# Weights of edges read by VectorE straight from the PSUM bank of the turned logits, in a graph-attention layer on one core

## The chip, the core and the metric

The kernel runs on one core of one Trainium2 chip. The metric is the device time of one execution in microseconds (us); lower is better. A time is the median of several executions, and the profile shows one execution of its own.

The core's engines have their own instruction queues, each worked off in order: TensorE (PE; its weight loads are listed as PEld), VectorE (DVE), ScalarE (ACT), GpSimd (POOL) and SyncE (SP). They wait for each other by semaphores. Data lies in SBUF, with 128 partitions, or in PSUM, where TensorE writes its products; PSUM consists of banks, and one bank holds 512 float32 numbers per partition.

## The reference, cut to what matters

```python
h = relu(layernorm(x))                          # 12500 nodes x 256
q, k, v = h @ Wq + bq, h @ Wk + bk, h @ Wv + bv # 8 heads of 32
logits  = einsum('ehd,ehd->eh', q[dst], k[src]) / sqrt(32)
seg_max = segment_max(logits, dst)
expv    = exp(logits - seg_max[dst])
denom   = segment_sum(expv, dst)
attn    = expv / denom[dst]
agg     = segment_sum(attn[:, :, None] * v[src], dst)
out     = agg + (h @ Wskip + bskip)
y       = h + gelu(out)
return x + layernorm(y) * gamma + beta
```

There are 200,000 edges, sorted by `dst`; `src` is random. So each edge fetches a row of k and v from anywhere, and its sums go to one of a few neighbouring nodes.

## The kernel before, in words

A first stage computes h and the tables of k and v and of q in DRAM. The last stage finishes what is left. Between them lies the *walk* over the edges, most of the span, and the change is there.

**Tiling.** The sorted edges are cut into S = 8 streams of NST = 66 steps. One step takes from each stream K = 3 tiles of 128 edges (two in the last step). An edge is a partition: a tile `kv` of 128 x 8 streams x 512 numbers holds k (first 256) and v (last 256) of 128 edges of each stream.

**One step c**, for its tiles j = 0, 1, 2:

- `gather` (L1027): GpSimd issues eight indirect DMAs per tile, two steps ahead, into one of six `kv` buffers; `gather_next(c, j)` fetches tile j of step c+2 into the buffer that `weigh(c, j)` has done with.
- `hot_e`, `hot_n` (L1042 to L1055): TensorE and ScalarE make 0/1 matrices that say which node an edge belongs to, `to_e` (node to edge) and `to_n` (edge to node).
- `spread` (L1065): TensorE spreads q over the edges, into PSUM (`ps_qe`); `times` (L1074): VectorE multiplies it into k, in place; `total` (L1081): VectorE reduces to logits `L`, 64 per edge partition (8 streams x 8 heads).
- `turn` (L1091): TensorE transposes the logits of a tile into the PSUM tile `ps_x`, partitions 0 to 63, 128 columns per tile. For j = 0 ScalarE then puts the previous step's last maximum into column 0 (L1093).
- `maxima` (L1102 to L1105): VectorE scans along the edges forward and backward, with `pen` marking the borders of nodes (scratch in partitions 64 to 127 of `ps_x`), and subtracts the maxima: `W`. `exponent` (L1109): ScalarE.
- `turn_back` (L1117): TensorE transposes the weights back to edges as partitions, 64 columns per tile, into columns 0 to 191 of `ps_x`.
- `weights` (L1125): ScalarE copies these 128 x 192 numbers into the SBUF tile `w`.
- `carried` (L1131, L1133): ScalarE copies what the previous step carried over (`wden`), and the weights of tiles 1 and 2 into the head columns of the products `vw`, since they also sum up to the denominators.
- `weigh` (L1140): VectorE multiplies v by the weights, broadcast over the 32 numbers of a head, into `vw`; for tile 0 a small multiply by `wden` follows (L1145).
- `add_up` (L1164): TensorE sums the products by nodes into `ps_a` (streams in group i = 0 and 2) and `ps_hot` (i = 1); ScalarE copies the sums (L1176) and puts the unfinished last node of each stream into the first row of the next step's tile (L1182); SyncE stores the sums.

Beside this a *pair* of finished node blocks is completed in about every 39/32 steps: divide (L841 to L855), skip product (L849, L862, L866), add (L871), gelu (L875), statistics (L878 on), and in the following step normalisation and scaling (L898 to L914).

**What sets the order.** No scheduler: the helper `keep` chains every instruction to the one before on its engine, so each engine's order is the order of the program text. The loop over c interleaves three steps by hand. In short: `times`, `total`, `turn` of (c, 2); `weigh(c-1, 2)`; `maxima(c)`; sums of c-1; `exponent(c)`; `turn_back(c)`; `weights(c)`; `carried(c)`; `times`, `total` of (c+1, 0); `weigh(c, 0)`; `hot_n(c)`; `turn(c+1, 0)`; the pair's middle part and `hot_e(c+2)`; `times`, `total`, `turn` of (c+1, 1); `weigh(c, 1)`; the rest of `hot_e(c+2)`; sums of (c, 0 and 1). Waits between engines come from the tiles: whoever reads a tile waits for its last writer, and a writer for its last readers, tracked by tile.

The buffers that matter: `w` has one, `ps_x` comes from a pool with one buffer, a whole bank; `turn(c, 0)` takes it anew in each step.

Of the kernel before, what the change touches and what calls it, by code (L numbers as in the profile page):

```python
# [28 lines left out]
F32 = mybir.dt.float32  # L29
# [11 lines left out]
P = 128  # L41
HEADS = 8
# [4 lines left out]
S = 8  # L47
K = 3
CH = K * P
# [709 lines left out]
def walk_streams(tc, N, HID, NST, KL, many, ident, idx, d0_row, slot_row, near, near_n, e_tab, pen_tab, h_tab,  # L759
# [6 lines left out]
    nc = tc.nc  # L766
# [3 lines left out]
    SH = S * HEADS  # L770
# [6 lines left out]
    def keep(ins):  # L777

        before = latest.get(ins.ins.engine)
        if before is not None:  # L780
            tc.add_manual_dep(ins.ins, before, mybir.DependencyInfo(
                mybir.DependencyClass.NoSync, mybir.DependencyReason.DATA), reason="kept order")
        latest[ins.ins.engine] = ins.ins.name
        return ins
# [167 lines left out]
    with ExitStack() as es:  # L952
        def pool_of(name, bufs, **kw):
            return es.enter_context(tc.tile_pool(name=name, bufs=bufs, **kw))
# [6 lines left out]
        work = pool_of("work", 2)  # L961
# [3 lines left out]
        xt_ps = pool_of("xt_ps", 1, space=PSUM)  # L965
# [22 lines left out]
        def tiles_of(c):  # L988
            return KL if c == NST - 1 else K


        step = [dict() for _ in range(NST + 3)]

        def where(s):
# [91 lines left out]
        def turn(c, j):  # L1086

            g = step[c]
            if j == 0:
                g["xt"] = xt_ps.tile([P, 512], F32, name="ps_x")  # L1090
            keep(nc.tensor.transpose(g["xt"][:SH, j * P:(j + 1) * P], g["L"][:, j, :], ident))  # L1091
            if j == 0:
                keep(nc.scalar.copy(g["xt"][:SH, 0:1],  # L1093
                                    low0 if c == 0 else step[c - 1]["M"][:, CH - 1:]))

        def maxima(c):
            g = step[c]
            n = tiles_of(c) * P
            X, R, pen = g["xt"][:SH, :n], g["xt"][SH:, :n], g["pen"]
            M = g["M"] = work.tile([SH, CH], F32, name="M")[:, :n]  # L1100
            W = g["W"] = work.tile([SH, CH], F32, name="W", bufs=1)[:, :n]
            keep(nc.vector.tensor_tensor_scan(R, pen[:SH, :n], X, -BIG, op0=OP.add, op1=OP.max))  # L1102
            keep(nc.vector.tensor_tensor_scan(mirrored(M, 0, n), mirrored(pen[SH:, :], 1, n),
                                              mirrored(R, 0, n), -BIG, op0=OP.add, op1=OP.max))
            keep(nc.vector.tensor_tensor(W, X, M, op=OP.subtract))  # L1105

        def exponent(c):
            W = step[c]["W"]
            keep(nc.scalar.activation(W, W, AF.Exp))  # L1109

        def turn_back(c):
            g = step[c]

            n = tiles_of(c)
            ps = g["xt"][:, :K * SH].rearrange("p (k n) -> p k n", k=K)
            for j in range(n):
                keep(nc.tensor.transpose(ps[:, j, :], g["W"][:, j * P:(j + 1) * P],  # L1117
                                         ident[:SH, :SH]))

        def weights(c):  # L1120
            g = step[c]
            n = tiles_of(c)
            ps = g["xt"][:, :K * SH].rearrange("p (k n) -> p k n", k=K)
            g["w"] = work.tile([P, K, SH], F32, name="w", bufs=1)
            keep(nc.scalar.copy(g["w"][:, :n, :], ps[:, :n, :]))  # L1125

        def carried(c):

            g = step[c]
            g["vw"] = [work.tile([P, S, SUMS], F32, name="vw", bufs=K) for _ in range(K)]  # L1130
            keep(nc.scalar.copy(wden[c % 2][0:1], g["kv"][0][0:1, :, HID - HEADS:HID]))  # L1131
            for j in range(1, tiles_of(c)):
                keep(nc.scalar.copy(g["vw"][j][:, :, :HEADS],  # L1133
                                    g["w"][:, j, :].rearrange("p (s h) -> p s h", s=S)))

        def weigh(c, j):
            g = step[c]
            t = g["vw"][j]
            wj = g["w"][:, j, :].rearrange("p (s h) -> p s h", s=S)
            keep(nc.vector.tensor_tensor(  # L1140
                t[:, :, HEADS:].rearrange("p s (h d) -> p s h d", h=HEADS),
                wj[:, :, :, None].to_broadcast([P, S, HEADS, D]),
                g["kv"][j][:, :, HID:].rearrange("p s (h d) -> p s h d", h=HEADS), op=OP.mult))
            if j == 0:
                keep(nc.vector.tensor_tensor(t[:, :, :HEADS], wj, wden[c % 2], op=OP.mult))  # L1145
# [100 lines left out]
        for c in range(NST - 1):  # L1246

            pair_next = None
            if c in due:
                pair_next = Pair(fin, due[c][0],  # L1250
                                 lambda: hot_ps.tile([P, 2, KC, P], F32, name="ps_hot"),
                                 lambda: ag_ps.tile([P, 2 * HID], F32, name="ps_a").rearrange(
                                     "p (b d) -> p b d", b=2),
                                 keep)
            if c + 2 < NST:
                windows(c + 2)
            for half in range(2):
                times(c, K - 1, half)
                spread(c + 1, 0, half)
            total(c, K - 1)  # L1260
            turn(c, K - 1)
            if c:
                weigh(c - 1, K - 1)
                gather_next(c - 1, K - 1)
            maxima(c)
            if before:
                before.factors()
            if c:
                add_up(c - 1, 0, range(K - 1, K))
                add_up_products(c - 1, 1)  # L1270
            exponent(c)
            turn_back(c)
            if c:
                add_up_results(c - 1, 1)
            weights(c)
            if c:
                add_up(c - 1, 2)
            carried(c)
            for half in range(2):
                times(c + 1, 0, half)  # L1280
                spread(c + 1, 1, half)
            total(c + 1, 0)
            weigh(c, 0)
            gather_next(c, 0)
            for j in range(K):
                hot_n(c, j)
            turn(c + 1, 0)
            if before:
                before.normal()
                before.shifted()  # L1290
            if pair:
                pair.turn()
                pair.divisors()
                pair.divide()
                pair.skip()
            if before:
                before.scale()
                before.store(0)
                before.store(1)
            if pair_next:  # L1300
                pair_next.fetch()
            if c == NST - 2:
                for i in range(4):
                    last(i)
            if c + 2 < NST:
                for i in range(QT // 2):
                    hot_e(c + 2, i)
            if pair:
                pair.add()
                table_of(AF.Gelu)  # L1310
                pair.gelu()
            for half in range(2):
                times(c + 1, 1, half)
                if tiles_of(c + 1) == K:
                    spread(c + 1, K - 1, half)
            total(c + 1, 1)
            turn(c + 1, 1)
            weigh(c, 1)
            gather_next(c, 1)
            if c + 2 < NST:  # L1320
                for i in range(QT // 2, QT):
                    hot_e(c + 2, i)
            add_up(c, 0, range(K - 1))
            if c + 2 < NST:
                penalties(c + 2)
            if c + 3 < NST:
                prefetch(c + 3)
            if c == NST - 2:
                weigh(c, K - 1)
                add_up(c, 0, range(K - 1, K))  # L1330
                add_up(c, 1)
                if pair_next:
                    pair_next.turn()
                    pair_next.skip()
            if pair:
                table_of(AF.Sqrt)
                pair.stats()
                pair.root()
                table_of(AF.Exp)
            if c == NST - 2:  # L1340
                add_up(c, 2)
            before, pair = pair, pair_next
            if c > 1:
                step[c - 2] = None

        c = NST - 1
# [14 lines left out]
        if before:  # L1361
            before.factors()
        turn_back(c)
        weights(c)
        carried(c)
        weigh(c, 0)
        if pair:
# [53 lines left out]
        if extra:  # L1421
            with tc.If(many > 0):
                for m in extra:
                    p = Pair(fin, m, lambda: hot_ps.tile([P, 2, KC, P], F32, name="ps_hot"),
                             lambda: ag_ps.tile([P, 2 * HID], F32, name="ps_a").rearrange(
                                 "p (b d) -> p b d", b=2), lambda ins: ins)
# [349 lines left out]
```

## Time and profile before

| | |
|---|---|
| median of 6 runs | 2954.03 us (2933.71 to 2965.32) |
| the profiled execution | 2965.96 us, its span 2964.2 us |
| mean granted TensorE clock in it | 0.678 |
| instructions in it | 29239 |
| data from and to HBM | 538.91 MB read, 108.23 MB written, 218 GB/s |
| `times` L1074 on VectorE | 394 of 1218 ns, 465.2 us |
| `total` L1081 on VectorE | 197 of 2286 ns, 450.4 us |
| `weigh` L1140 on VectorE | 197 of 2285 ns, 450.1 us |
| gathers L1027 on GpSimd | 1576 of 1099 ns, 1731.3 us |

A group of the profile is written as line, engine, operation, output <- inputs, shapes, x count; then the busy time in us, the mean of one in ns, and after a second bar the time in which the engine stood idle just before such an instruction, with what ended it. "remote" is a releaser that the profile can't name, "issue" stands for no wait that the profile shows. A wait line gives total us, how often, and the longest. A timeline line gives start and duration in us, and in brackets the idle time before it. Matmul ends are modelled.

### The profile page before, as it was taken

What the parts mean: (1) busy time and instruction counts of PE and PEld (TensorE: products, weight loads), DVE (VectorE), ACT (ScalarE), POOL (GpSimd) and SP (SyncE); (2) the same over time, 40 slices, a digit from 0 to 9 for tenths busy, and PEclk for the clock granted to TensorE, in tenths of its full rate; (3) what the DMA queues carried; (4) which work ended last, traced back from release to release, by engine and by line L of the source; (5) the groups of instructions that cost most, each with busy time, mean ns of one, the idle gap of its engine ahead of it and who ended that gap; (6) DMA issues with size and microseconds to landing.
All of it is one profiled execution on the core that took longest, in us unless ns stands there. A gap on an engine that the chain in (4) does not pass through costs nothing.

```text
span 2964.2 us, 29239 instructions
## 1 busy us (share of the span) xinstructions
PE 1796.3 (61%) x7824; PEld 941.0 (32%) x7824; DVE 1989.8 (67%) x2330; ACT 1099.8 (37%) x2552; POOL 1868.7 (63%) x1745
## 2 busy tenths in 40 slices
PE   6899824445454756565565556667665666555556
PEld 3455412212232323233233323333332333223333
DVE  7777546666575767667666667767776766756774
ACT  3333212222243434434334434334344444334343
POOL 4423557776775766677576676676766776756750
PEclk9999856665576566656766666665666666666677
DMA  7766766676776777777677777787776776867762
GB/s 249 266 236 254 255 187 206 204 214 201 220 232 192 226 229 224 207 228 226 194 223 219 222 233 226 223 241 226 231 222 204 234 226 210 251 186 225 228 196 86
DMA packets 306127, 649.33 MB, mean 219 GB/s; under 512 B 52836, under 2 KB 192238, under 8 KB 300954
## 3 DMA queue, kind: packets, MB, share of 16 engines
q0 software_dynamic: 128768, 423.23, 48.5%
q1 hardware_dynamic: 176434, 223.46, 22.9%
q8 instruction: 65, 1.06, 0.1%
q14 instruction: 112, 0.92, 0.1%
q10 hardware_dynamic: 748, 0.66, 0.1%
HBM read 538.91 MB, written 108.23 MB: 218 GB/s over the span
## 4 chain that ended last, share of the span: by engine, by line
PE 26%; another core or an unknown queue 20%; issue 17%; ACT 12%; DVE 11%; POOL 8%; DMA 4%; SPq 1%; DVEq 0%; POOLq 0%; ACTq 0%
POOL kv L1027 7%; PE ps_kv L256 4%; PE ps_a L1164 4%; DVE vw L1140 3%; ACT kv L1182 3%; DVE kv L1074 3%; PE ps_qe L1065 3%; PE ps_a L866 3%; PE ps_hot L908 2%; PE ps_q L262 2%; DMA kv<-kv_tab,idx 2%; PE ps_hot L1164 2%; ACT to_e L1044 2%; PE ps_hot L1053 1%
## 5 line engine op out<-in xcount | busy, mean ns | idle before, releaser
L1027 POOL DMA_INDIRECT kv<-kv_tab,idx x1576 | 1731.3, 1099 | 794.7 <-issue 456.0
L1140 DVE TENSOR_TENSOR vw<-w,kv 128x2048 f32<-128x2048 f32 x197 | 450.1, 2285 | 414.1 <-ACT kv L1182 288.8
L1074 DVE TENSOR_TENSOR kv<-ps_qe,kv 128x1024 f32<-128x1024 f32 x394 | 465.2, 1218 | 97.6 <-remote 42.6
L1081 DVE TENSOR_REDUCE L<-kv 128x64 f32<-128x2048 f32 x197 | 450.4, 2286 | 6.9 <-issue 0.2
L1164 PE MATMUL ps_a<-vw,to_n 128*32 128x264 f32 (+1 forms) x2344 | 322.8, 556 | 103.0 <-DVE vw L1140 58.0
L1065 PE MATMUL ps_qe<-qw,to_e 64*128 64x256 f32 (+1 forms) x1576 | 319.8, 403 | 106.5 <-issue 83.5
L1053 PE MATMUL ps_hot<-near_n,et 48*128 48x384 bf16 x197 | 71.5, 400 | 455.5 <-issue 200.8
L1176 ACT COPY sums_w<-ps_a 128x264 f32<-128x264 f32 x130 | 49.4, 380 | 786.6 <-remote 441.9
L1044 ACT ACTIVATE to_e<-ps_hot,ones 128x384 fp32r<-128x384 f32 x396 | 213.2, 579 | 338.8 <-PE ps_hot L1042 147.8
L1065 PEld LDWEIGHTS ps_qe<-qw,to_e 64*128 64x128 f32 (+1 forms) x1576 | 230.1, 256 | 266.5 <-issue 203.5
L1042 PE MATMUL ps_hot<-et,near 48*128 48x384 bf16 x396 | 144.5, 417 | 119.8 <-issue 83.3
L1164 PEld LDWEIGHTS ps_a<-vw,to_n 128*32 128x32 f32 (+1 forms) x2344 | 113.4, 153 | 308.4 <-issue 169.8
L256 PE MATMUL ps_kv<-w_kv,hT 128*128 128x512 f32 x392 | 192.4, 612 | 17.2 <-ACT hT L141 15.5
L268 POOL TENSOR_TENSOR qp<-qp 128x256 fp32r<-128x256 f32 x98 | 88.5, 903 | 167.5 <-ACT qp L267 167.1
L1164 PE MATMUL ps_hot<-vw,to_n 128*64 128x264 f32 x808 | 188.5, 616 | 8.7 <-issue 8.2
L1091 PEld LDWEIGHTS ps_x<-ident,L 128*64 128x64 f32 x197 | 24.6, 125 | 511.5 <-issue 475.5
L1102 DVE TENSOR_TENSOR_SCAN ps_x<-pen,ps_x 64x384 f32<-64x384 f32 x66 | 63.0, 955 | 177.3 <-remote 123.0
L986 ACT ACT_TABLE_LOAD x138 | 177.1, 1283 | 2.4
L1117 PE MATMUL ps_x<-ident,W 64*128 64x64 f32 x197 | 35.4, 309 | 214.0 <-ACT W L1109 153.2
L866 PE MATMUL ps_a<-w_s,hT 128*128 128x256 f32 x368 | 144.9, 562 | 11.1 <-issue 3.3
L1055 ACT ACTIVATE to_n<-ps_hot,ones 128x384 f32<-128x384 f32 x197 | 107.0, 579 | 105.7 <-remote 91.2
L1182 ACT COPY kv<-ps_a 1x264 f32<-1x264 f32 x388 | 143.2, 369 | 6.3
(279 smaller groups left out, 2229.2 us busy)
## 6 DMA issues: line engine op xcount, KB each, us to landing
qw<-q_pc SPq DMA_DIRECT2D x264, 128.0 KB
kv<-kv_tab,idx POOLq DMA_INDIRECT x1576
kv_tab<-kvo SPq DMA_DIRECT2D x16, 1280.0 KB
q_pc<-qp SPq DMA_DIRECT2D x16, 1280.0 KB
qw<-q_pc SPq DMA_DIRECT2D x264, 64.0 KB
table<-sums_w SPq DMA_DIRECT2D x264, 61.9 KB
pen<-pen_tab SPq DMA_DIRECT2D x66, 192.5 KB
sums<-table SPq DMA_DIRECT2D x92, 132.0 KB
```

The lines of the kernel that those rows point to most:

```text
L256: ins = nc.tensor.matmul(ps_kv, hT[:, c, :], w_kv[:, c, :], start=c == 0, stop=c == KC - 1)
L866: self.keep(nc.tensor.matmul(self.ps[:, b, :], self.hT[:, b, c, :], w_s[:, c, :], start=False, stop=False, skip_group_check=True))
L986: keep(nc.scalar.activation(dummy[:, 1:2], dummy[:, 0:1], function))
L1027: nc.gpsimd.indirect_dma_start(out=t[:, s, :], out_offset=None, in_=kv_tab[:, :], in_offset=bass.IndirectOffsetOnAxis(ap=idx[:, s, j, c:c ...
L1042: keep(nc.tensor.matmul(ps[:, :CH], near[:, i * P:(i + 1) * P], step[c]["et"], start=True, stop=True))
L1044: keep(nc.scalar.activation(step[c]["to_e"][:, i, :], ps[:, :CH], AF.Relu, scale=-1.0, bias=ones))
L1065: keep(nc.tensor.matmul(ps[:, b, a, :], g["to_e"][at:at + w, i, j * P:(j + 1) * P], g["qw"][at:at + w, i, :], start=True, stop=True))
L1074: keep(nc.vector.tensor_tensor(k, g["qe", half].rearrange("p b a d -> p a b d"), k, op=OP.mult))
L1081: keep(nc.vector.tensor_reduce(g["L"][:, j, :].rearrange("p (s h) -> p s h", s=S), g["kv"][j][:, :, :HID].rearrange("p s (h d) -> p s h d" ...
L1140: keep(nc.vector.tensor_tensor(t[:, :, HEADS:].rearrange("p s (h d) -> p s h d", h=HEADS), wj[:, :, :, None].to_broadcast([P, S, HEADS, D] ...
L1164: keep(nc.tensor.matmul(ps[at:at + w, :], g["to_n"][:, j, i * P + at:i * P + at + w], g["vw"][j][:, s, :], start=j == 0, stop=j == tiles_o ...
L1182: keep(nc.scalar.copy(step[c + 1]["kv"][0][0:1, s, HID - HEADS:], ps[at:at + 1, :]))
```

## The change

One tile `turned`, a whole bank of 512 columns, is taken once for the whole walk in place of a new `ps_x` tile in each step. Logits and scratch stay in columns 0 to 383. The transposed-back weights of tile 0 go to columns 0 to 63 as before, those of tile 1 to columns 384 to 447 and of tile 2 to columns 448 to 511, outside the columns of the logits. The copy to `w` (L1125) is dropped; `carried` and `weigh` read the weights in PSUM. In the changed kernel `weigh` is L1133, its small multiply L1138, the copies into the head columns L1127, `turn` L1091, `maxima` L1102.

```diff
+        turned = xt_ps.tile([P, CH + 2 * SH], F32, name="ps_x")
...
         def turn(c, j):
             g = step[c]
+            keep(nc.tensor.transpose(turned[:SH, j * P:(j + 1) * P], g["L"][:, j, :], ident))
             if j == 0:
-                g["xt"] = xt_ps.tile([P, 512], F32, name="ps_x")
-            keep(nc.tensor.transpose(g["xt"][:SH, j * P:(j + 1) * P], g["L"][:, j, :], ident))
-            if j == 0:
-                keep(nc.scalar.copy(g["xt"][:SH, 0:1],
+                keep(nc.scalar.copy(turned[:SH, 0:1],
                                     low0 if c == 0 else step[c - 1]["M"][:, CH - 1:]))
...
-            X, R, pen = g["xt"][:SH, :n], g["xt"][SH:, :n], g["pen"]
+            X, R, pen = turned[:SH, :n], turned[SH:, :n], g["pen"]
...
+        def weight(j):
+            at = CH + (j - 1) * SH if j else 0
+            return turned[:, at:at + SH].rearrange("p (s h) -> p s h", s=S)
+
         def turn_back(c):
-            ps = g["xt"][:, :K * SH].rearrange("p (k n) -> p k n", k=K)
-            for j in range(n):
-                keep(nc.tensor.transpose(ps[:, j, :], g["W"][:, j * P:(j + 1) * P],
-                                         ident[:SH, :SH]))
-
-        def weights(c):
-            g = step[c]
-            n = tiles_of(c)
-            ps = g["xt"][:, :K * SH].rearrange("p (k n) -> p k n", k=K)
-            g["w"] = work.tile([P, K, SH], F32, name="w", bufs=1)
-            keep(nc.scalar.copy(g["w"][:, :n, :], ps[:, :n, :]))
+            for j in range(tiles_of(c)):
+                keep(nc.tensor.transpose(weight(j).rearrange("p s h -> p (s h)"),
+                                         step[c]["W"][:, j * P:(j + 1) * P], ident[:SH, :SH]))
...
             for j in range(1, tiles_of(c)):
-                keep(nc.scalar.copy(g["vw"][j][:, :, :HEADS],
-                                    g["w"][:, j, :].rearrange("p (s h) -> p s h", s=S)))
+                keep(nc.scalar.copy(g["vw"][j][:, :, :HEADS], weight(j)))
...
         def weigh(c, j):
-            wj = g["w"][:, j, :].rearrange("p (s h) -> p s h", s=S)
+            wj = weight(j)
...
             turn_back(c)
             if c:
                 add_up_results(c - 1, 1)
-            weights(c)
             if c:
                 add_up(c - 1, 2)
             carried(c)
```

The same call is dropped in the last step, which stands outside the loop.

More of the change, by code (lines that the diff above doesn't have):

```diff
@@ L1109, in exponent @@
             keep(nc.scalar.activation(W, W, AF.Exp))
+        def weight(j):
+            at = CH + (j - 1) * SH if j else 0
+            return turned[:, at:at + SH].rearrange("p (s h) -> p s h", s=S)
         def turn_back(c):
-            g = step[c]
-            n = tiles_of(c)
-            ps = g["xt"][:, :K * SH].rearrange("p (k n) -> p k n", k=K)
-            for j in range(n):
-                keep(nc.tensor.transpose(ps[:, j, :], g["W"][:, j * P:(j + 1) * P],
-                                         ident[:SH, :SH]))
-        def weights(c):
-            g = step[c]
-            n = tiles_of(c)
-            ps = g["xt"][:, :K * SH].rearrange("p (k n) -> p k n", k=K)
-            g["w"] = work.tile([P, K, SH], F32, name="w", bufs=1)
-            keep(nc.scalar.copy(g["w"][:, :n, :], ps[:, :n, :]))
+            for j in range(tiles_of(c)):
+                keep(nc.tensor.transpose(weight(j).rearrange("p s h -> p (s h)"),
+                                         step[c]["W"][:, j * P:(j + 1) * P], ident[:SH, :SH]))
         def carried(c):
@@ L1363, in walk_streams @@
         turn_back(c)
-        weights(c)
         carried(c)
```

## The prediction

> **What bounds the kernel now.** First the page's busy times, then its costliest groups. A step of the walk lasts some 38.5 us on average; VectorE works for 29 us of it, so no engine is full, and the time is set by who waits for whom.
>
> ```profile
> PE 1796.3 (61%) x7824; PEld 941.0 (32%) x7824; DVE 1989.8 (67%) x2330; ACT 1099.8 (37%) x2552; POOL 1868.7 (63%) x1745
> ```
>
> The groups of instructions by line give the copy that goes and its neighbours, and the price of a VectorE pass with and without a PSUM operand.
>
> ```profile
> L1140 DVE TENSOR_TENSOR vw<-w,kv 128x2048 f32<-128x2048 f32 x197 | 450.1, 2285 | 414.1 <-ACT kv L1182 288.8 <-issue 71.4 <-ACT sums_w L1176 48.4
> L1125 ACT COPY w<-ps_x 128x192 f32<-128x192 f32 x66 | 21.0, 318 | 28.2 <-PE ps_hot L1053 12.7 <-remote 11.2 <-PE ps_x L1117 1.3
> L912 DVE TENSOR_TENSOR sums<-sums,gam 128x512 f32<-128x512 f32 x46 | 31.7, 688 | 41.1 <-ACT sums L898 41.1
> L914 DVE TENSOR_TENSOR o<-sums,ps_hot 128x512 f32<-128x512 f32 x46 | 31.6, 687 | 20.1 <-PE ps_hot L908 17.8 <-DVE sums L912 1.6
> ```
>
> The copy is small, and next to nothing waits in front of it. The list of waits shows where VectorE stands still: before the weighing, for ScalarE's carry copies, and before the maxima, for TensorE.
>
> ```profile
> DVE vw L1140 <- ACT kv L1182: 288.8, 38, 18.4
> DVE ps_x L1102 <- remote: 123.0, 25, 14.5
> ACT sums_w L1176 <- remote: 566.0, 69, 19.9
> ```
>
> ScalarE itself waits 566 us at the copy of the sums (L1176), which stands in its queue a few instructions before L1125. "remote" names no releaser; in some 60 of 64 steps the first of these waits is for TensorE's sums. Matmul ends are modelled, and users of TensorE's results often see them microseconds later than the record: the maxima started that way in 41 of 65 steps, by a median of 4.9 us.
>
> Last the timeline of one step (35), VectorE and TensorE, columns start and duration:
>
> ```profile
> 1777.52 2.29 DVE L1140 TENSOR_TENSOR vw<-w,kv 128x2048 f32<-128x2048 f32 x1 [10.46 <-ACT kv L1182]
> 1779.73 0.22 DVE L1145 TENSOR_TENSOR vw<-w,wden 128x64 f32<-128x64 f32 x1
> ...
> 1785.11 2.29 DVE L1081 TENSOR_REDUCE L<-kv 128x64 f32<-128x2048 f32 x1
> 1787.31 2.28 DVE L1140 TENSOR_TENSOR vw<-w,kv 128x2048 f32<-128x2048 f32 x1
> 1789.51 0.68 DVE L878 TENSOR_TENSOR sums<-sums,h 128x512 f32<-128x512 f32 x1
> ```
> ```profile
> 1779.12 0.42 PE L1091 MATMUL ps_x<-ident,L 128*64 128x128 f32 x1
> ...
> 1788.86 0.27 PE L1091 MATMUL ps_x<-ident,L 128*64 128x128 f32 x1
> ```
>
> Here the weighing of the current step (L1140) and the turning of the next step's logits (L1091) run side by side. They can, because the weighing reads SBUF while the turn writes the PSUM bank.
>
> **What the change removes.** 66 copies L1125 of 318 ns, 21 us of ScalarE. In 56 of 66 steps ScalarE waits for TensorE before its next copy of sums, so what it saves it waits there again: I take 0, with −21 us as the other end. GpSimd's next gather loses a wait for ScalarE; its true condition, the end of the weighing, stays. SyncE's order does not change.
>
> **What it adds: waits on one bank.** In the built programs each engine keeps its order, but the waits differ. Weights, logits and scan scratch now share one tile that lives for the whole walk and fills one bank, and dependencies go by the tile. Whoever reads weights must wait for a turn that comes before it in the program, and a turn for the weighing before it. Four edges follow.
>
> *First weighing (tile 0).* It waited for the last carry copy L1182; now it waits for ScalarE's second copy into the head columns (L1133, now from PSUM), 0.53 us after the old start in each step's records. This delays VectorE by 0.53 us wherever it stood waiting there. I count it in the next item.
>
> *Turn of the next step's tile 0 (TensorE).* It now waits for the small multiply L1145 behind the first weighing. Queued behind the turn on TensorE are the shift and skip products of the pair (L905, L862), the hot matrices of step c+2 (L1042) and the spread for tile 2. Step 35: L1145 ends at 1779.95, plus 0.53 and 0.05 for the hand-off, against the turn's start at 1779.12: 1.41 us. The same subtraction over 63 full steps, negative ones set to zero, gives 47 us, 42.5 of it from 30 steps. The other end is 0: TensorE is busy for 61% and may make it up.
>
> *Second weighing (tile 1).* It had no wait. Now it waits for the turn of the next step's tile 1, which waits for the reduce right ahead of the weighing on VectorE: a round trip through TensorE's queue, with VectorE standing. Step 35: the turn ends at 1789.13, with 0.04 for the hand-off 1.86 us after the weighing's old start. Over the 63 steps this is 203 us, 3.2 a step. VectorE idled after that weighing for some of it anyway; taking that off step by step leaves 118. Next comes the wait before the maxima (L1102), 164 us over all, into which the delay is pushed where it stood: that leaves 53. Queued behind are the pair's add and statistics, the next times and reduce, and the gather of tile 1, which waits for this weighing. I take 53, with 118 as the upper end.
>
> *Third weighing (tile 2, previous step's buffers).* Likewise it now waits for the turn of the current step's tile 2. It used to run while TensorE got there, and the maxima then found the turn done or nearly. Step 17:
>
> ```profile
> 1095.83 2.29 DVE L1081 TENSOR_REDUCE L<-kv 128x64 f32<-128x2048 f32 x1
> 1098.03 2.28 DVE L1140 TENSOR_TENSOR vw<-w,kv 128x2048 f32<-128x2048 f32 x1
> 1100.53 0.96 DVE L1102 TENSOR_TENSOR_SCAN ps_x<-pen,ps_x 64x384 f32<-64x384 f32 x1 [0.22 <-PE ps_x L1091]
> ```
> ```profile
> 1100.08 0.41 PE L1091 MATMUL ps_x<-ident,L 128*64 128x128 f32 x1
> ```
>
> VectorE spent the 2.28 us of the weighing inside TensorE's delay. Afterwards the order is turn, weighing, maxima, so the whole 2.28 us stands on the path. 38 steps had a wait before the maxima over 0.1 us: 38 × 2.28 = 87 us. In the other 25 only the round trip is new, some 0.6 us: 14 us. Together 101. TensorE's next task, the sums of tile 2, also starts from this weighing, but in steps where the sums came late by TensorE's own work (L1176 follows the maxima by more than the usual 1.31 us) the delay meets idle time; that absorbs 34. I take 67, between 14 and 101.
>
> **What costs nothing.** The weighing reads its 64 weights per partition from PSUM. L912 and L914 are one shape, without and with a PSUM operand: 688 and 687 ns, so 0. The transposes back only change columns. Gathers start 2 to 3 us later; they are issued two steps ahead, and VectorE waited only 21.3 us in 7 places for gathered data. If that cover went, GpSimd's 24 gathers of 1.099 us and their gaps of 0.3, 33.6 us a step, would be next to bound, still below 38.5.
>
> [...]
>
> **The sum.** 0 + 47 + 53 + 67 = +167 us. The profiled execution lasted 2965.96 us (span 2964.2 and 1.8 around it), so it would become 3133. It lies 12 us above the median of the six runs, 2954.03; on that median I forecast 3121. Lower end: the round trips of the second weighing (53) and of the third (14), the turn hidden, the copies gained: 53 + 14 − 21 = +46, 3000. Upper end: 47 + 118 + 101 = 266, and 15 us of measurement: 3235.
>
> **Rivals.** *Hidden:* the new waits fall into those that stand already (288.8 us before L1140, 123 before L1102), because TensorE or ScalarE is late whatever VectorE does. Then only the 0.53 us at the first weighing is paid: 66 × 0.53 = 35, less 21, 2968. For it speaks that the times of users show TensorE later than its records; against it, that a late TensorE makes the round trips longer, and they begin only when VectorE has finished its reduce.
>
> *Faster:* 38 and 11 waits of the weighing, 288.8 and 48.4 us, end on ScalarE, and L1125 stands in front of the copies there. If that is the chain, the walk gains all of 66 × 0.318: 2933 us. It decides as soon as the new waits cost less than 21 / 66 = 0.32 us a step. Against it: the round trip from reduce over turn to weighing has a transpose of 0.27 to 0.42 us plus two hand-offs, and it comes twice a step.
>
> *Heavier:* TensorE's real lateness, not its records, rules the new waits, nothing is absorbed, and the delay passes from step to step: 47 + 203 + 101 = 351, 3305; it counts as such from 3235. For it: 566 us of ScalarE waiting for TensorE. That the change does not do what it says is excluded by the program's order: the copy is gone.
>
> **How the numbers follow.** The forecast case, 3000 to 3235, has 0.80; hidden, below 3000, 0.07; faster 0.03; heavier 0.10. Left out are 2 in 10. About 0.5%, 15 us, is what a measurement of this kernel can tell from no change: of the hidden case 0.04 lies within that and 0.03 above it. So faster 0.03, same 0.04, slower 0.93.
>
> **What would show it.** In the profile after: no copy of 128x192 on ScalarE; new waits of the weighing for TensorE's turn of the logits, some 130 of them, 1 to 4 us each; fewer and shorter waits before the maxima; the turn waiting for VectorE's small multiply; the weighing still at 2.28 us; VectorE's busy sum unchanged. I am wrong if the weighing itself is longer, if waits for gathered data grow beyond 21 us, or if the weighing's idle time on TensorE stays under 50 us.

## The result, and the profile after

The changed kernel takes 3209.22 us (median of 20 runs, 3199.03 to 3230.33) against 2950.64 us (46 runs): ratio 1.0895, 95% interval 1.0874 to 1.0916, 259 us slower. The profiled execution has a span of 3200.6 us, 236 us more than that of before. One thing has to be known to read the rest: runs sent together ran on one chip, and chips differ. On the later occasions, on three chips, the kernel before took 3028 us (the single weighings below), 2725 us (called the second chip) and 3013 us (called the third), so only ratios within one occasion are compared. The chip of the result is not on record, and each chip was seen on one occasion, so "chip" here stands for chip and occasion together. The ratios leave out executions more than 1.5% above the fastest of their kernel, so they need not be the quotient of the medians beside them, and the trace of the run r1 below is of such an execution.

The page's busy times of the changed kernel:

```profile
PE 1847.3 (58%) x7824; PEld 954.9 (30%) x7824; DVE 2000.0 (62%) x2330; ACT 1086.6 (34%) x2486; POOL 1647.0 (51%) x1745
```

ScalarE has 66 instructions less, VectorE's work is 10 us more, and GpSimd, at the same number of instructions, is busy for 222 us less. Two of the costliest groups:

```profile
L1029 POOL DMA_INDIRECT kv<-kv_tab,idx x1576 | 1509.8, 958 | 1245.5 <-issue 446.8
L1133 DVE TENSOR_TENSOR vw<-ps_x,kv 128x2048 f32<-128x2048 f32 x197 | 451.4, 2292 | 934.7 <-ACT vw L1127 507.3
```

The weighing reads PSUM at 2292 ns (2285 from SBUF). Idle time before it has gone from 414.1 to 934.7 us. A gather takes 958 ns in the mean, where it took 1099. The list of waits (total us, times, longest):

```profile
ACT sums_w L1169 <- remote: 615.6, 65, 21.2
DVE vw L1133 <- ACT vw L1127: 507.3, 64, 10.7
...
DVE vw L1133 <- PE ps_x L1091: 174.3, 43, 5.9
DVE vw L1133 <- remote: 166.5, 21, 11.0
...
DVE ps_x L1102 <- remote: 12.2, 1, 12.2
```

The wait before the maxima (123.0 us before) is all but gone; in its place stand waits of the weighing for the turn, named or as "remote". The largest is the first weighing's, for the chain that ends with ScalarE's copy into the head columns. One step in the timeline of VectorE, and the turn of tile 1 on TensorE (L1091):

```profile
1895.64 2.29 DVE L1083 TENSOR_REDUCE L<-kv 128x64 f32<-128x2048 f32 x1
1901.10 2.29 DVE L1133 TENSOR_TENSOR vw<-ps_x,kv 128x2048 f32<-128x2048 f32 x1 [3.17 <-PE ps_hot L1044]
...
1907.38 2.29 DVE L1083 TENSOR_REDUCE L<-kv 128x64 f32<-128x2048 f32 x1
1910.18 2.29 DVE L1133 TENSOR_TENSOR vw<-ps_x,kv 128x2048 f32<-128x2048 f32 x1 [0.52 <-issue]
1912.51 0.96 DVE L1102 TENSOR_TENSOR_SCAN ps_x<-pen,ps_x 64x384 f32<-64x384 f32 x1
...
1917.71 2.29 DVE L1083 TENSOR_REDUCE L<-kv 128x64 f32<-128x2048 f32 x1
1929.27 2.29 DVE L1133 TENSOR_TENSOR vw<-ps_x,kv 128x2048 f32<-128x2048 f32 x1 [9.27 <-ACT vw L1127]
```
```profile
1899.31 0.27 PE L1091 MATMUL ps_x<-ident,L 128*64 128x128 f32 x1
```

The second weighing stands 3.17 us behind its reduce, the third 0.52 us, with the scan right behind it: the two round trips as forecast. (The profile puts the first of these waits down to L1044, the product that follows the turn on TensorE; by the records the turn itself ended 1.52 us before the weighing began.) Then VectorE idles for 9.27 us. What ScalarE does in that time, and the last of the gathers of that tile on GpSimd:

```profile
1915.43 0.52 ACT L1109 ACTIVATE W<-W 64x384 f32<-64x384 f32 x1
1926.52 0.38 ACT L1169 COPY sums_w<-ps_hot 128x264 f32<-128x264 f32 x1 [10.57 <-remote]
```
```profile
1922.70 0.95 POOL L1029 DMA_INDIRECT kv<-kv_tab,idx  x1 [0.30 <-issue]
1931.83 0.95 POOL L1029 DMA_INDIRECT kv<-kv_tab,idx  x1 [8.17 <-DVE den L841]
```

ScalarE waits 10.57 us for sums whose last matmul, by its modelled end, was over at 1916.5. It goes on 2.87 us after the last gather was issued, about when its rows have landed (the gather's semaphore counts up at 1925.8). Of 125 waits of over 3 us at this copy, 42 end 1.9 to 3.1 us after the end of a tile's last gather; on the second chip it is 1 of 66. In the same stretch SyncE's register instructions, 0.03 us as a rule, take 0.7 us.

Where the time went, by stages of the step, from VectorE's records (mean us over 62 steps; "second chip" and "no gathers" are runs told of below):

| stage | before | after | after, second chip | before, no gathers | after, no gathers |
|---|---|---|---|---|---|
| first weighing to end of reduce, tile 1 | 9.85 | 9.72 | 9.72 | 8.77 | 9.35 |
| from there to second weighing | -0.08 | 3.64 | 2.98 | -0.08 | 2.80 |
| to end of reduce, tile 2 | 10.11 | 8.05 | 8.50 | 7.96 | 7.97 |
| from there to the scan | 4.82 | 5.13 | 2.84 | 2.12 | 2.84 |
| scan to W | 2.53 | 2.54 | 2.54 | 2.53 | 2.53 |
| W to the next first weighing | 11.41 | 13.05 | 5.47 | 4.94 | 5.42 |
| step | 38.65 | 42.13 | 32.04 | 26.23 | 30.92 |

From before to after a step grows by 3.48 us: 1.66 at the second weighing (3.72 of wait, 2.06 of it given back by the stage behind), 0.31 up to the scan, 1.64 from W to the next first weighing, less 0.13. Times 62 it is 216 us of the 236.

### The profile page after: what moved, and what is told of

It reads as the page before. It is cut to its first block, busy times and chain, and to the rows that moved or that the text cites. A ratio compares the mean times of both kernels' runs of the same rounds, so it can differ in the third digit from the quotient of the medians.

```text
span 3200.6 us, 29136 instructions
## 1 busy us (share of the span) xinstructions
PE 1847.3 (58%) x7824; PEld 954.9 (30%) x7824; DVE 2000.0 (62%) x2330; ACT 1086.6 (34%) x2486; POOL 1647.0 (51%) x1745
## 4 chain that ended last, share of the span: by engine, by line
PE 24%; another core or an unknown queue 23%; issue 18%; DVE 16%; ACT 10%; POOL 4%; DMA 4%; DVEq 0%; ACTq 0%; POOLq 0%; SPq 0%
DVE vw L1133 5%; ACT kv L1175 4%; DVE L L1083 4%; PE ps_kv L256 4%; DVE kv L1076 3%; POOL kv L1029 3%; PE ps_qe L1067 3%; PE ps_hot L908 3%; PE ps_a L866 2%; PE ps_a L871 2%; DMA kv<-kv_tab,idx 2%; PE ps_a L1157 2%; PE ps_q L262 2%; ACT sums_w L1169 2%
## 5 line engine op out<-in xcount | busy, mean ns | idle before, releaser
L1029 POOL DMA_INDIRECT kv<-kv_tab,idx x1576 | 1509.8, 958 | 1245.5 <-issue 446.8
L1133 DVE TENSOR_TENSOR vw<-ps_x,kv 128x2048 f32<-128x2048 f32 x197 | 451.4, 2292 | 934.7 <-ACT vw L1127 507.3
L1157 PE MATMUL ps_a<-vw,to_n 128*32 128x264 f32 (+1 forms) x2344 | 305.1, 538 | 323.6 <-DVE vw L1133 297.1
L1067 PE MATMUL ps_qe<-qw,to_e 64*128 64x256 f32 (+1 forms) x1576 | 327.4, 410 | 148.3 <-issue 130.4
L1067 PEld LDWEIGHTS ps_qe<-qw,to_e 64*128 64x128 f32 (+1 forms) x1576 | 237.6, 262 | 303.5 <-issue 242.5
L1157 PEld LDWEIGHTS ps_a<-vw,to_n 128*32 128x32 f32 (+1 forms) x2344 | 96.0, 142 | 504.8 <-DVE vw L1133 339.6
L1044 PE MATMUL ps_hot<-et,near 48*128 48x384 bf16 x396 | 151.2, 444 | 77.3 <-ACT to_e L1046 52.3
L1091 PE MATMUL ps_x<-ident,L 128*64 128x128 f32 x197 | 78.9, 400 | 190.7 <-DVE vw L1138 96.7
L1169 ACT COPY sums_w<-ps_hot 128x264 f32<-128x264 f32 x68 | 25.7, 378 | 465.2 <-remote 453.9
L866 PE MATMUL ps_a<-w_s,hT 128*128 128x256 f32 x368 | 159.0, 605 | 8.7 <-ACT hT L852 2.9
L1091 PEld LDWEIGHTS ps_x<-ident,L 128*64 128x64 f32 x197 | 25.0, 127 | 425.0 <-DVE vw L1138 305.5
L866 PEld LDWEIGHTS ps_a<-w_s,hT 128*128 128x128 f32 x368 | 106.5, 304 | 53.0 <-issue 17.4
```

What stands on the lines that cost most here:

```text
L866: self.keep(nc.tensor.matmul(self.ps[:, b, :], self.hT[:, b, c, :], w_s[:, c, :], start=False, stop=False, skip_group_check=True))
L1029: nc.gpsimd.indirect_dma_start(out=t[:, s, :], out_offset=None, in_=kv_tab[:, :], in_offset=bass.IndirectOffsetOnAxis(ap=idx[:, s, j, c:c ...
L1044: keep(nc.tensor.matmul(ps[:, :CH], near[:, i * P:(i + 1) * P], step[c]["et"], start=True, stop=True))
L1067: keep(nc.tensor.matmul(ps[:, b, a, :], g["to_e"][at:at + w, i, j * P:(j + 1) * P], g["qw"][at:at + w, i, :], start=True, stop=True))
L1133: keep(nc.vector.tensor_tensor(t[:, :, HEADS:].rearrange("p s (h d) -> p s h d", h=HEADS), wj[:, :, :, None].to_broadcast([P, S, HEADS, D] ...
L1157: keep(nc.tensor.matmul(ps[at:at + w, :], g["to_n"][:, j, i * P + at:i * P + at + w], g["vw"][j][:, s, :], start=j == 0, stop=j == tiles_o ...
```

## Experiments

**One weighing at a time.** The kernel before with the persistent tile and the weights at columns 320 to 511; the copy to `w` is kept, and only the weighings named read PSUM. The runs are called r1, r2, r0 and r012 after the weighings that read PSUM. What the persistent tile costs by itself, with all weighings from SBUF, was not tried.

```diff
             wj = g["w"][:, j, :].rearrange("p (s h) -> p s h", s=S)
+            if j in (1,):      # (2,), (0,), (0, 1, 2)
+                wj = turned[:, CH + (j - 1) * SH:CH + j * SH].rearrange("p (s h) -> p s h", s=S)
```

> The copy to SBUF is kept and everything but the second weighing (tile 1) reads it; the second reads PSUM. Theory (what counts is how late the third weighing starts, and the round trip through TensorE's turn of the next tile 1 delays the second and so the third): second weighing 3.2 us a step later, of which 1.5 to 2 remain, so 2951 + 95 to 130, about 3060. Rival A (TensorE is late there only because its turn of tile 0 is held up by the first weighing): with the first weighing on SBUF the wait shrinks, 2951 + 20 to 50. Rival B (reading PSUM costs by itself): + 5 us at most.

Measured: ratio 1.0253 (1.0195 to 1.0311) to 3027.55 us, +77 us. Between theory and rival A, below the theory's 95; the interval is 59 to 94 us. The wait is there: 3.13 us in the mean behind the reduce.

> Copy kept; only the third weighing (tile 2, previous step) reads PSUM. Theory: it waits for the turn of the current tile 2, 0.5 us in most steps and several in some (mean 2.9 in the changed kernel), and all that TensorE does for the sums follows: 2951 + 100 to 160. The prediction's sum gave 67 (14 to 101) for this. Rival C (the maxima waited for that turn anyway and the weighing only slips behind it): 2951 + 0 to 30.

Measured: 1.0362 (1.0323 to 1.0400), +110 us, as the theory said; rival C is out. The third weighing starts 4.99 us behind its reduce in the mean, and the scan 7.31 us.

> Copy kept; only the first weighing (tile 0) and its small multiply read PSUM, so TensorE's turn of the next tile 0 waits for the small multiply; the head columns are still copied from SBUF. The prediction's sum gave 47 (0 to 47) for this. Theory now: TensorE catches up, 2951 + 0 to 20. Rival A: 2951 + 50 or more, since all of TensorE's queue behind the turn is late.

Measured: 1.0143 (1.0100 to 1.0186), +43 us. The theory's 0 to 20 fell; 43 (interval 30 to 56) is about what the prediction's sum had (47), and rival A's 50 is not excluded. In its profile `times`, which needs TensorE's spread, waits 149.6 us in 26 places for a releaser that isn't named (42.6 us in 13 places in the profile before); the spread stands behind the turn.

> All three weighings read PSUM, but the copy to SBUF is kept and feeds the head columns. Against the changed kernel this keeps 0.32 us of ScalarE work a step and drops the wait of the first weighing for the head-column copies (0.53 us a step). Theory: the copy itself is worth nothing, the head-column wait 20 to 35 us, so 3175 to 3215, 2951 + 225 to 265. If the sum of the three single runs is less than this, the waits strengthen each other.

Measured: 1.0653 (1.0613 to 1.0693), +198 us: less than forecast and less than the three single runs together (230). So the waits do not strengthen each other; that they overlap is likely, but 32 us is hardly more than the intervals of the four ratios leave open.

**The turns behind the weighings; no gathers.** In the changed kernel two calls change places, which makes the run s12:

```diff
-            turn(c, K - 1)
             if c:
                 weigh(c - 1, K - 1)
                 gather_next(c - 1, K - 1)
+            turn(c, K - 1)
...
-            turn(c + 1, 1)
             weigh(c, 1)
             gather_next(c, 1)
+            turn(c + 1, 1)
```

and, in both kernels, the gathers from step 2 on are left out:

```diff
+            if c > 1 and j < len(first[c % 2]):
+                step[c].setdefault("kv", []).append(first[c % 2][j])
+                return
             t = gath.tile([P, S, KV], F32, name="kv")
+            first[c % 2].append(t)
```

> The changed kernel itself, on the same chip as the runs sent with it, for r012_copy_kept and the others to be held against. With r012 at a ratio of 1.065: if the head-column wait of 0.53 us a step stands on the path, the changed kernel lies some 35 us above r012, ratio 1.075 to 1.09; if the gone copy of 0.32 us a step pays for it, it is the same, 1.06 to 1.07.

Measured: 0.9336 (0.9318 to 0.9354): 2544.28 against 2725.47 us, *faster* by 181 us. Neither outcome that was written down. It is the same program as in the result, on another chip (the second). The run with the copy kept was not repeated there, so what the head columns and the gone copy are worth in the full kernels stays open.

> The changed kernel with two turns moved in the program: the turn of tile 1 behind the second weighing, the turn of tile 2 behind the third. Then these weighings have nothing to wait for, and TensorE waits 2.3 us for them instead. Theory (the late start of the second and third weighing is the cost): most comes back, before + 0 to 60, ratio 1.00 to 1.02; the maxima start a weighing and a round trip behind the reduce, 2.9 us, where before they started 4.8 us behind it on average. Rival (any serial use of the one bank costs it, whoever waits): ratio 1.04 to 1.08.

Measured: 0.8935 (0.8918 to 0.8952), 2434.93 us, 291 us below before and outside both forecasts. Against the changed kernel on that chip the moved turns gain 109 us. A step takes 30.33 us, and GpSimd's 24 gathers of 958 ns with gaps of 0.30 us make 30.2. From step 2 on each of the 1528 gathers follows the one before it within 0.35 us: GpSimd is the bound.

> The kernel before without the gathers of the walk from step 2 on: the six tiles of k and v are used again and again (the result is that of other data). Theory G (the sums' signals from TensorE come only when the gather in flight has landed, so gathers set the pace): 38.6 us a step falls to about 30, so 2300 to 2550 us. Theory R (round trips between engines alone): 2800 or more, since VectorE waited only 21 us for gathered data.

> The changed kernel, likewise without the gathers from step 2 on. Theory G (the new waits cost so much because they delay the gather that waits for the third weighing, and the sums' signals wait for its landing): the difference to nb_no_gathers is well below the 258 us of the full kernels, 60 to 150 us, that of the bare round trips. Theory R: the difference stays at 200 to 260.

Measured: 2172.46 us for before and 2468.05 for the changed kernel (ratios 0.797 and 0.9054 to the full kernel before). Both pages, before first:

```profile
PE 1566.5 (72%) x7824; PEld 825.9 (38%) x7824; DVE 1966.1 (90%) x2330; ACT 1096.5 (50%) x2552; POOL 187.6 (9%) x217
```
```profile
PE 1751.7 (71%) x7824; PEld 916.2 (37%) x7824; DVE 1990.1 (80%) x2330; ACT 1083.1 (44%) x2486; POOL 183.0 (7%) x217
```

Without gathers before is bound by VectorE (90%), and the change opens gaps there: 296 us, above both forecasts. So theory G was wrong that gathers make the waits dear: the bare waits alone cost 296 us, where with gathers the change saves 181 us on this chip. The table's last two columns split it, per step: 0.58 up to the end of the reduce of tile 1 (the held turn), 2.88 for the second weighing, 0.72 up to the scan, 0.48 from W to the first weighing (the head columns). G was right that gathers set the pace of the kernel before: they cost it 553 us here, and the changed kernel only 76. The 2172 us lie below G's 2300 to 2550, though, and that gathers do so by late signals, as G has it, is doubtful here: before was not traced with gathers on this chip, and the changed kernel's trace, below, shows no late signal.

What gathers gain by the change is to be read in the profile of before already, in the timeline of GpSimd beside the weighing shown in the prediction, which began at 1787.31 and ended at 1789.59:

```profile
1787.21 0.95 POOL L1027 DMA_INDIRECT kv<-kv_tab,idx  x1 [0.30 <-issue]
1788.47 1.96 POOL L1027 DMA_INDIRECT kv<-kv_tab,idx  x1 [0.30 <-issue]
1790.73 0.95 POOL L1027 DMA_INDIRECT kv<-kv_tab,idx  x1 [0.30 <-issue]
```

The gather that began within the weighing lasted 1.01 us longer and ended 0.84 us behind it. Before, 178 of 1576 gathers took over 1.2 us, in all 231 us above 0.953 us each; after, on the first chip, none did, 9.5 us in all. All 149 gathers that began within a weighing from SBUF took 1.9 to 3.0 us; all 79 that began within a weighing in the changed kernel took under 0.97 us. Of the other 29 stretched ones, 26 began within the divide (L855), whose two operands also lie in SBUF. Mean times of a gather go with the number of weighings that read SBUF: 1099 ns with three, 1065, 1062 and 1013 with two (r0, r1, r2), 972 with none.

On this second chip the changed kernel's waits are these:

```profile
DVE vw L1133 <- PE ps_x L1091: 224.5, 129, 5.4
...
DVE vw L1133 <- ACT vw L1127: 44.4, 62, 5.7
```

and ScalarE at the place where it stood for 10.57 us:

```profile
1507.14 0.52 ACT L1109 ACTIVATE W<-W 64x384 f32<-64x384 f32 x1
1508.23 0.38 ACT L1169 COPY sums_w<-ps_hot 128x264 f32<-128x264 f32 x1 [0.57 <-PE ps_hot L1157]
```

Here all 129 waits for the turn carry their releaser's name, "remote" is gone, and the sums are seen 0.57 us after the exponent. Of 1922 register instructions of SyncE none takes 0.2 us; on the first chip 294 do (260 for before).

**Again, on a third chip.** The weighing from SBUF with the moved turns (the diff above, made in the kernel before) is new; the others are repeated.

> The changed kernel once more, as the measure for the runs sent with it, on whatever chip they get. The first comparison gave a ratio of 1.09 on a chip where the kernel before takes 2951, the second 0.93 on a chip where it takes 2725. If the chip decides the sign (how late TensorE's signals come while gathers are in flight), the ratio is 0.93 to 0.95 where before takes some 2725, and 1.05 to 1.09 where it takes 2950 or more.

Measured: 1.0656 (1.0581 to 1.0731), 3226.40 against 3013.25 us: the sign of the first chip, as was forecast for such a time of before.

> Both turns behind the weighings, weights in PSUM. Where before takes some 2725: 2435 again, GpSimd bound (24 gathers of 1.26 us, 30.2 us a step). Where before takes 2950 or more: theory (round trips and gathers each have their share) 2750 to 2950, faster than before; rival (there the late signals rule everything) 3000 or more.

Measured: 1.1110 (1.1036 to 1.1183), 3364.54 us: the rival's case, and slower than the changed kernel itself, by 138 us. The waits of the maxima, here first and on the second chip next:

```profile
DVE ps_x L1102 <- remote: 788.0, 49, 20.8
```
```profile
DVE ps_x L1102 <- PE ps_x L1091: 32.9, 65, 0.6
```

In this order the maxima wait for a turn that starts behind the third weighing, at the moment when that weighing sets the next gathers off. On the second chip this wait is 0.5 us a time, here 16 us in 49 steps.

> The kernel before with the copy and the weighing from SBUF, but with the two turns behind the weighings as in s12: what of s12's gain is the order, and what the operand in PSUM. Theory (a VectorE pass with both inputs in SBUF holds up GpSimd's gathers, 231 us in the profile before and 10 in the one after): 24 x 1.4 us of GpSimd a step, 100 to 230 us above s12. Rival (the gain is the order of the turns): within 30 us of s12.

Measured: 0.9986 (0.9934 to 1.0038), 3019.85 us: no difference to before, and 345 us *below* s12, which on this chip had no gain to split. The run says less than was meant. The turn is TensorE's and the weighing VectorE's, so moving one call past the other changes the order on no engine; it only decides which of the two waits for the other, and with the weights in SBUF neither does. The traces bear this out: engine by engine, the run has the same instructions with the same waits as before. So it is the kernel before once more, and what of s12's gain on the second chip is the direction of the wait, and what the operand in PSUM, stays open. The gathers are held up as in before:

```profile
L1027 POOL DMA_INDIRECT kv<-kv_tab,idx x1576 | 1725.3, 1095 | 857.5 <-issue 457.2
```

> The changed kernel without the gathers from step 2 on, again. Where before takes some 2725: 2468 as measured. Where before takes 2950 or more: 2460 to 2500 too if the chips differ only in what gathers in flight do to the signals; 2650 or more if they differ without gathers as well.

Measured: 2477.66 us, against 2468.05 on the second chip. Without gathers the two chips agree within 0.4%; with them the changed kernel takes 3226 here and 2544 there. With gathers, 57 of 153 waits for TensorE's sums at their copy end here over 5 us behind the modelled end of the last matmul (55 of 153 on the first chip); on the second chip none of 197 does, and here without gathers none of 193. So on this chip it is the gathers that make the signals late. It is not that their transfers are slower, as the gathers' queue shows (packets, MB, share of the 16 DMA engines; second chip first, then here):

```profile
q0 software_dynamic: 128768, 423.23, 55.3%
```
```profile
q0 software_dynamic: 128768, 423.23, 43.6%
```

Of spans of 2541.8 and 3227.2 us that is 1406 and 1407 us. One more number differs: with gathers the mean granted TensorE clock is 0.702 there and 0.657 here, without them 0.712 and 0.720. Whether this is cause or consequence is not shown; TensorE's busy time, 1763.8 and 1826.8 us, differs by 63 of the 682 us.

## Why the prediction was right, and where it was not

The forecast was 3121 with a range of 3000 to 3235; measured is 3209, high in the range. The direction and the mechanism held on this chip: waits on the one bank, in the second and third weighing above all. There is luck in the hit. The same program was 181 us faster on another chip, and the terms miss both ways and partly cancel. Put into the stages of the table, in us over the walk, the forecast was +47 for the held turn, +118 at the second weighing, 101 - 65 = +36 up to the scan (65 is what the wait before the maxima was to swallow), and -34 behind W; measured are -8, +103, +19 and +102. Point by point, against +47, +53, +67:

- **The held turn, 47.** Right in size alone (43 in r0, 0.58 us a step or 37 without gathers), but in the full change on the first chip the stage is 0.13 us *shorter*. That TensorE has run dry and catches up when the first weighing comes late for the sums would fit; no run shows it. The head columns' 0.53 us, put into the same item, show as 0.48 us without gathers.
- **The second weighing, 53.** The raw delay was right: 3.72 us a step measured, 3.2 forecast. So was the first deduction: 1.66 us a step remain, 103 us, against 118. The second deduction, 65 us into the wait before the maxima, is not borne out where this weighing stands alone: r1 costs 77 us, and in its trace the scan stands 6.30 us behind its reduce, against 4.82 in the profile before. In the full change the third weighing sees the turn 2.81 us behind the reduce and then fills the gap, so that the scan stands at 5.13; how much of the delay the gap swallowed cannot be told apart there.
- **The third weighing, 67.** Up to the scan the forecast was large enough, 36 against 19. The step that failed is the deduction of 34, for sums that came late "by TensorE's own work": behind W there are not 34 us less but 102 more, of which the head columns would be 33 at 0.53 us a step. Alone the third weighing costs 110 us. On this chip a third of the waits for the sums ends about when a gather has landed (42 of 125), and the third weighing sets gathers off; that a later weighing therefore moves the sums too is a reading, not shown by a run of its own.
- **What costs nothing: gathers.** The step that was missed. They were looked at as starting later, not as running freer. The trace shows it: 231 us of stretched gathers before, 9.5 after, and the mean of 1099 ns against the usual 953 stood in the page that the prediction read. What the stretching goes with, the two traces show as well: of the gathers that began within a weighing, all 149 were stretched, to 1.9 to 3.0 us, where both its inputs lay in SBUF, and none of 79, all under 0.97 us, where one lay in PSUM. The freed gathers are a gain for the change; that on the second chip it is what outweighs the waits is argued below.
- **PSUM as operand, 0.** Right within 7 ns (2292 against 2285): 1.4 us for the 197 weighings, and 0.5 us for 66 of them, where rival B of r1 allowed up to 5.
- **VectorE's work.** The 29 us a step were too many: 1619 us of VectorE in 2400 us of the walk (470 to 2870) are 26 us a step. Nothing in the sum rests on it. Of the prediction's signs of being wrong none came on the first chip: the weighing takes 2292 ns, and VectorE waits 16.0 us for gathered data.

Of the rivals, *faster* came true on one chip, by 181 us, but not through ScalarE's chain; its price and condition were those of the copy, and no run shows what the copy alone is worth. *Heavier* had put the bare waits at 351; without gathers they are 296. *Hidden* is out on every chip.

What is shown: the waits and their sizes (r0 to r012, the pair without gathers), the freed gathers (durations in every trace), and that gathers make signals late on the third chip and not on the second (the runs with and without gathers). Why chips differ is open, and so is which part of a signal is slow; that SyncE's register instructions slow down in the same stretches says only that it is not TensorE alone. How much of the 181 us is the freed GpSimd was not tried by itself on the second chip; that, as an estimate, before is at 24 x (1.099 + 0.30) = 33.6 us of GpSimd in a step of some 34.9 there (26.23 us without gathers, plus 553 / 64; the 1.099 us are from the first chip's trace) speaks for it.

## What to carry to other kernels

Before a copy out of PSUM is dropped, list who writes that bank next: the copy's worth was not its 0.3 us but that it let the bank go, and here the readers left behind made the next write a round trip (at the second weighing, 2.88 us a step without gathers and 3.72 with them on the first chip). When an idle gap is to swallow a delay, ask who sets its end: here the stretch behind W did not swallow 34 us of the delay but grew by 102. And look at the other side of an operand's move: a VectorE pass with one input in PSUM left GpSimd's gathers alone here (none of 79 stretched, against 149 of 149). And before two calls are swapped to learn something, see whether they share an engine or a tile; if not, the program stays the same (a ratio of 0.9986, where the turns moved past weighings from SBUF).

## What the runs showed of the hardware that was not expected

The same two programs stand at 1.0895, 0.9336 and 1.0656 on three occasions. On the first and the third, ScalarE sees TensorE's sums over 5 us behind the modelled end of their last matmul in 55 and 57 of 153 waits, and some 300 of SyncE's 1922 register instructions take 0.7 us for 0.03; on the second neither happens, and on the third without gathers no sum is that late and 10 register instructions are slow. Without gathers the changed kernel takes 2468 us on the second and 2478 us on the third. A comparison on one chip can have the wrong sign for another.
